# A graph layer on one core: the rows of x by a transpose, and lists, flag and bases moved

## The chip, the cores and the metric

The kernel runs on one core of a Trainium2 chip. The metric is the device time of one execution in microseconds (us); the time before is a median of three runs. Beside these runs there is one profiled execution with its own time and trace.

## The reference

There are 50,000 nodes with 128 numbers each (x) and 1,650,000 edges, sorted by their target. Each edge takes the row of its source, sends it through one of two linear maps (chosen by the edge's type), and the results are added up at the target. Then follow the node's own linear map, a relu, the sum with x, and a normalisation of each row:

```python
msg = jnp.where((edge_types == 0)[:, None], Xs @ W_data.T + b_data, Xs @ W_control.T + b_control)   # Xs = X[src]
agg = jax.ops.segment_sum(msg, dst, num_segments=X.shape[0])
out = relu(agg + (X @ W_self.T + b_self))
return _layernorm(X + out)
```

## The kernel before, in words

The sum over edges comes first and the linear maps after it, since both are linear. The edges are cut into 503 blocks of some 3,284. A block's edges end in a window of 112 nodes, whose first node is the block's base. Three ways bring the source rows of a block into SBUF:

- 24 chunks of 128 edges are gathered by POOL (GpSimd), one indirect DMA each (`gathers`, L464). Their lists of row numbers come from `fill`, which DVE runs five blocks ahead (`RAHEAD`). The rows land in a pool of ten buffers `y` of six chunks each.
- 128 edges are fetched as single rows, one DMA of 512 B each, half by SP's queue and half by ACT's (`single_rows`, L440). The row offsets are loaded into registers, 32 at a time (L435), and the rows are fetched two blocks ahead (`AHEAD`) into `yx`.
- Up to 84 edges are loops from a node to itself. They are left out of the lists and added from the window's own columns `xT` (`left_out_*`, L336 to L361).

For each chunk DVE makes a one-hot matrix over target and type (`onehot`, L401) and counts (`counts`, L409), and PE multiplies it with the rows into `acc` (L483, L489). DVE adds `acc` into one of three buffers `sums` (`add`, L499), which is carried from block to block with a shift (`begin_sums`, L512). When a block's sum is complete, `layer` multiplies it with the weights on PE into `po` (L517 to L520), `moments` takes relu and the sum with x on DVE (`h`, L525) and the moments (L527, L529), `root` takes the square root on ACT (L534), and `store` normalises (L540, L542) and writes the rows out by SP's queue (L543).

The order is written out by hand (`manual_schedule`): each engine runs its instructions in the order in which the loop over blocks issues them, and a DMA is issued in its queue's order. In an iteration b the loop first calls `window(b + 3)`, which reads the base of that block into a register of SP (L387) and loads the 112 rows `xw` (L393) and the same nodes' columns `xT` (L395, from a transposed copy of x). Then come the block's four passes of six chunks, and between them `layer(b - 1)`, `moments(b - 1)`, `onehot(b + 2)`, `counts(b + 2)`, `store(b - 1)`, `fill(b + 5)` and `single_rows(b + 2)`.

Before the loop, three weights are loaded, transposed on PE (L910) and copied (L911). Their buffers `w_sb` are given back, and the tiles that `straight` allocates next reuse the memory. `idx0`, the list of block 0, is the first DMA of SP (L116). After the loop a flag is computed (L618 to L640): it says whether the edges were as regular as this path assumes. All engines read it (L919), and only if it is above zero does a slower general path run. In the execution shown it does not run.

Of the kernel before, what the change touches and what calls it, by code (L numbers as in the profile page):

```python
# [11 lines left out]
F32 = mybir.dt.float32  # L12
# [4 lines left out]
ALU = mybir.AluOpType  # L17
# [5 lines left out]
N = 50000  # L23
D = 128
# [60 lines left out]
def straight(ctx, tc, c, x, x_t, src_t, dst_t, etype_t, src_f, dst_f, etype_f, src_x, dst_first, first_p, out):  # L85
# [38 lines left out]
    num_ps, rank_no_ps = small[:, :2 * W], small[:, 2 * W:2 * W + F]  # L124
    lists = [small[:, 2 * W + F + i * FILL:][:, :FILL] for i in range(2)]
    sums_at = [small[:Q * F, 2 * W + F + 2 * FILL + i:][:, :1] for i in range(2)]
    nc.vector.tensor_copy(num_ps, num)

    ones_b = keep.tile([P, P], BF16, name="ones_b")
    nc.vector.memset(ones_b, 1.0)  # L130
# [1 line left out]
    below = keep.tile([P, P], BF16, name="below")  # L132
    nc.gpsimd.affine_select(out=below, in_=ones_b, pattern=[[1, P]], compare_op=ALU.is_gt, fill=0.0,
                            base=0, channel_multiplier=-1)
    rank_no = keep.tile([P, F], F32, name="rank_no")
    nc.vector.tensor_scalar(rank_no, num[:, :F], -LOOP, None, op0=ALU.add)
    nc.vector.tensor_copy(rank_no_ps, rank_no)
# [243 lines left out]

    idxs = {0: idx0}
    bys, pcs, zs, pls, bases, ats, ys = {}, {}, {}, {}, {}, {}, {}
    ohs, cnts, accs, xws, xTs, pos, hs, mvs, sds = {}, {}, {}, {}, {}, {}, {}, {}, {}

    def base_of(b):
        return nc.values_load(base_i[0:1, b:b + 1], engines=[SP], min_val=0, max_val=N - B,  # L387
                              skip_runtime_bounds_check_because="it was clamped to this")

    def window(b):  # L390
        at = bases[b] = base_of(b)
        xw = stp.tile([B, D], F32, name="xw", bufs=5)
        nc.sync.dma_start(xw, x[bass.ds(at, B), :])  # L393
        xT = stp.tile([P, B], F32, name="xT", bufs=5)
        nc.sync.dma_start(xT, x_t[:, bass.ds(at, B)])  # L395
        xws[b], xTs[b] = xw, xT

    def onehot(b):
        g, i = divmod(b, GB)
# [13 lines left out]

    ROW_SLOTS = AHEAD + 2
    TURN = S // 2
    LOAD = TURN // 1
    RANGE = dict(min_val=0, max_val=(N - 1) * ROW, skip_runtime_bounds_check_because="where a node's row is")
    x_bytes = x.rearrange("n d -> (n d)").bitcast(U8)[None, :]
    fetched = [[tc.alloc_semaphore(f"fetched{j}_{i}") for i in range(ROW_SLOTS)] for j in range(2)]
# [5 lines left out]
            ats[b] = stp.tile([1, X], I32, name="at_x", bufs=AHEAD + 2)  # L425
            nc.vector.tensor_scalar(ats[b], one_g[g][:, i * X:(i + 1) * X], float(ROW), None, op0=ALU.mult)

    def single_rows(b, q, part):

        if q == 0 and part == 0:  # L430
            ys[b] = stp.tile([S, Q, D], F32, name="yx", bufs=ROW_SLOTS)
        both = []
        for j, (eng, dma) in enumerate(((SP, nc.sync), (ACT, nc.scalar))):
            at = j * TURN + part * LOAD
            _, rows = nc.values_load_multi_w_load_instructions(  # L435
                ats[b][0:1, q * S + at:q * S + at + LOAD], engines=[eng], **RANGE)
            both.append([(dma, fetched[j][b % ROW_SLOTS], at + k, row) for k, row in enumerate(rows)])
        for pair in zip(*both):
            for dma, sem, k, row in pair:
                copy = dma.dma_start(ys[b][k:k + 1, q, :].bitcast(U8), x_bytes[:, bass.ds(row, ROW)])  # L440
                copy.then_inc(sem, 16)
                tc.no_tile_sem_insts.add(copy.ins.name)
                tc.add_to_no_dep_group(f"single{b}", copy.ins)
# [69 lines left out]

    def layer(b):
        a = sums[b % RING]
        po = ps_o.tile([B, D], F32, name="po")
        nc.tensor.matmul(po, xTs.pop(b), c["wselfT"], start=True, stop=False)  # L517
        nc.tensor.matmul(po, a[0:3, 2, :B], bias, start=False, stop=False)  # L518
        for t in range(2):
            nc.tensor.matmul(po, a[:, t, :B], c["wmsgT"][:, t * D:(t + 1) * D], start=False, stop=t == 1)  # L520
        pos[b] = po

    def moments(b):
        h = stp.tile([B, D], F32, name="h")
        nc.vector.scalar_tensor_tensor(h, pos.pop(b), 0.0, xws.pop(b), op0=ALU.max, op1=ALU.add)  # L525
        st = stp.tile([B, 6], F32, name="st")
        nc.vector.bn_stats(st, h)  # L527
        mv = stp.tile([B, 2], F32, name="mv")
        nc.vector.bn_aggr(mv, st)  # L529
        hs[b], mvs[b] = h, mv  # L530
# [6 lines left out]
    def store(b):  # L537
# [4 lines left out]
        nc.vector.tensor_scalar(o, hs.pop(b), mv[:, 0:1], rstd, op0=ALU.subtract, op1=ALU.mult)  # L542
        nc.sync.dma_start(out[bass.ds(bases.pop(b), B), :], o)  # L543

    for b in range(1, AHEAD + 1):
        offsets(b)
    columns(0)
# [6 lines left out]
    for b in range(1, RAHEAD):  # L554
        fill(b)
        left_out_columns(b)
        left_out_matrix(b)
        if b < AHEAD:
            onehot(b)
            counts(b)  # L560
            for q in range(Q):
                for part in range(1):
                    single_rows(b, q, part)
        if b == 1:
            clear_sums()
    for b in range(NBLK + 1):
        if b + 3 < NBLK:
            window(b + 3)
        g, i = divmod(b, GB)
        if i == 0 and g + 1 < GROUPS:  # L570
            load_edges(g + 1)
        if i == 3 and g + 1 < GROUPS:
            spread_out(g + 1)
        if i == 4 and g + 1 < GROUPS:
            spread_in(g + 1)
        if b > 0:
            add(b - 1, steps_of(b - 1)[-1])
        if b < NBLK:
            begin_sums(b)
        last = steps_of(b)[-1:]  # L580
        for q, (step, ks) in enumerate(passes_of(b)):
            if ks:
                products(b, step, ks)
            if q == 0 and b > 0:
                layer(b - 1)
            if q == 1:
                left_out_numbers(b + 1)
            if q == 3:
                left_out_columns(b + RAHEAD)
            if ks and step not in last and ks[-1] == chunks_of(b, step)[-1]:  # L590
                add(b, step)
            if q == 0 and b > 0:
                moments(b - 1)
            if q == 0 and b + AHEAD < NBLK:
                onehot(b + AHEAD)
            if q == 1 and b > 0:
                root(b - 1)
            if q == 2 and b > 0:
                store(b - 1)
            if q == 1 and b + AHEAD < NBLK:  # L600
                counts(b + AHEAD)
            if q == 2 and i == 2 and g + 1 < GROUPS:
                columns(g + 1)
            if q == 2:
                left_out_rows(b + 1)
                if b + RAHEAD < NBLK:
                    fill(b + RAHEAD)
            if q == 3:
                left_out_matrix(b + RAHEAD)
                offsets(b + AHEAD + 1)  # L610
            if q % 2 == 0 and not plain(b + AHEAD):
                single_rows(b + AHEAD, q // 2, 0)


    ones = keep.tile([P, 1], F32, name="ones")
    nc.vector.memset(ones, 1.0)
    mm = keep.tile([P, 2], F32, name="mm")
    nc.vector.tensor_reduce(mm[:, 0:1], stats[:, :, 0, :], AX.XY, ALU.min)  # L618
    nc.vector.tensor_reduce(mm[:, 1:2], stats[:, :, 1, :], AX.XY, ALU.max)
    bad = keep.tile([P, 3], F32, name="bad")  # L620
    least = keep.tile([P, 1], F32, name="least")
    nc.vector.tensor_reduce(least, loops, AX.X, ALU.min)
    nc.vector.tensor_scalar(bad[:, 2:3], least, float(F), None, op0=ALU.is_lt)
    nc.vector.tensor_scalar(bad[:, 0:1], mm[:, 0:1], 0.0, None, op0=ALU.is_lt)
    nc.vector.tensor_scalar(bad[:, 1:2], mm[:, 1:2], float(W), None, op0=ALU.is_ge)
    gap = keep.tile([1, 3], F32, name="gap")
    nc.vector.tensor_reduce(gap[:, 0:1], shift, AX.X, ALU.min)
    nc.vector.tensor_reduce(gap[:, 1:2], shift, AX.X, ALU.max)
    nc.vector.tensor_scalar(gap[:, 0:1], gap[:, 0:1], 0.0, None, op0=ALU.is_lt)
    nc.vector.tensor_scalar(gap[:, 1:2], gap[:, 1:2], float(B), None, op0=ALU.is_gt)  # L630
    pb = ps_o.tile([B, D], F32, name="po")
    nc.tensor.matmul(pb[:3, 0:1], bad, ones, start=True, stop=True)
    both = keep.tile([3, 1], F32, name="both")
    nc.vector.tensor_copy(both, pb[:3, 0:1])
    pc = ps_o.tile([B, D], F32, name="po")
    nc.tensor.matmul(pc[:1, 0:1], both, ones[:3, 0:1], start=True, stop=True)
    nc.vector.tensor_copy(gap[:, 2:3], pc[:1, 0:1])
    total = keep.tile([1, 1], F32, name="total")
    nc.vector.tensor_reduce(total, gap, AX.X, ALU.add)
    nc.vector.tensor_copy(c["bad"], total)  # L640


def general(ctx, tc, c, x, src, dst, etype, out):
# [221 lines left out]
def gnn_resnorm(  # L865
# [35 lines left out]
    nc.vector.memset(eps, EPS)  # L901
    wmsgT = const.tile([P, 2 * D], F32, name="wmsgT")
    wselfT = const.tile([P, D], F32, name="wselfT")
    with tc.tile_pool(name="wts", bufs=2) as wts, \
            tc.tile_pool(name="wts_ps", bufs=2, space=bass.MemoryType.PSUM) as wts_ps:
        for w, o in ((w_data, wmsgT[:, :D]), (w_ctrl, wmsgT[:, D:]), (w_self, wselfT)):
            w_sb = wts.tile([P, D], F32, name="w_sb")
            nc.scalar.dma_start(w_sb, w)
            pw = wts_ps.tile([P, D], F32, name="pw")
            nc.tensor.transpose(pw, w_sb, ident)  # L910
            nc.scalar.copy(o, pw)  # L911
# [63 lines left out]
```

## Time and profile before

| | us |
|---|---|
| median of three runs | 24,102.25 |
| the three runs | 24,035.24, 24,102.25, 24,134.87 |
| the profiled execution's own time | 15,118.55 |
| its span | 15,116.8 |
| POOL busy, DVE busy | 11,399.7, 10,626.1 |
| PE busy, granted TensorE clock | 8,042.1, 0.544 |

The span runs from the first instruction to the last. Busy time counts instructions of the engine itself and neither its waits nor the issue of DMAs by SP and ACT. In the rows of instruction groups, the number after the bar is the busy time, then the mean duration in ns, then the idle time of the engine just before those instructions and what ended most of it. The profiled execution is much shorter than the runs shown, and nothing in the page says why; both are given wherever it matters.

### The profile page before, as it was taken

To read this page: it belongs to the slowest core of one execution; us is meant where nothing else is said; L and a number is where in the kernel's file an instruction comes from. 1 tells how busy PE (TensorE), PEld (TensorE's weight loads), DVE (VectorE), ACT (ScalarE), POOL (GpSimd) and SP (SyncE) were. 2 spreads that over 40 slices of the span, in tenths; PEclk is the share of its full clock that TensorE was granted. 3 is DMA by queue.
4 is the path that set the end of the run, shared out by engine and by line. 5 is a ranking of instruction groups with operands and counts; after the bars stand their busy time and mean duration, and the time that the engine had idled before them with its cause. 6 is when DMAs were issued, how large, how long until landed. Compare 5 with 4: busy or idle time off the path is not lost.

```text
span 15116.8 us, 243274 instructions
## 1 busy us (share of the span) xinstructions
PE 8042.1 (53%) x34836; PEld 6872.7 (45%) x34837; DVE 10626.1 (70%) x13316; ACT 151.7 (1%) x509; POOL 11399.7 (75%) x12071
## 2 busy tenths in 40 slices
PE   3555555555555555555555555555555555555555
PEld 3444444444444444444444444444444444444444
DVE  8776676767767767776676767767777676767765
ACT  0000000000000000000000000000000000000000
POOL 7777777777777777777777777777777777777777
PEclk7555555555555555555555555555555555555555
DMA  2332222222222222222222222222222222222222
GB/s 66 64 65 64 65 65 64 64 65 65 64 65 64 65 64 65 64 65 64 65 64 65 64 65 64 65 64 65 65 64 64 65 65 64 64 65 65 64 65 58
DMA packets 753407, 970.59 MB, mean 64 GB/s; under 512 B 355317, under 2 KB 552100, under 8 KB 751779
## 3 DMA queue, kind: packets, MB, share of 16 engines
q0 software_dynamic: 385968, 791.19, 21.5%
q1 hardware_dynamic: 301244, 146.99, 4.0%
q10 hardware_dynamic: 64566, 16.74, 0.6%
q14 instruction: 1345, 11.01, 0.2%
q8 instruction: 284, 4.65, 0.1%
HBM read 924.76 MB, written 29.02 MB: 63 GB/s over the span
## 4 chain that ended last, share of the span: by engine, by line
POOL 59%; issue 20%; PE 9%; DMA 6%; DVE 4%; ACTq 1%; SPq 0%; POOLq 0%; PEldq 0%; ACT 0%; PEld 0%; DVEq 0%
POOL y L464 59%; DMA y<-in_x,idx 6%; PE acc L483 6%; PE po L520 2%; PE po L518 1%; PE po L517 1%; ACTq L440 1%; DVE cnt L409 0%; DVE by L329 0%; DVE h L525 0%; DVE st L527 0%; DVE m L310 0%; DVE new L313 0%; DVE v_new L317 0%; DVE old L326 0%
## 5 line engine op out<-in xcount | busy, mean ns | idle before, releaser
L464 POOL DMA_INDIRECT y<-in_x,idx x12048 | 11385.9, 945 | 3683.0 <-issue 3573.7
L483 PE MATMUL acc<-oh,y 128*128 128x120 f32 x24122 | 5753.1, 428 | 6277.9 <-PEq L471 6263.0
L483 PEld LDWEIGHTS acc<-oh,y 128*128 128x128 f32 x24122 | 5208.8, 325 | 6688.2 <-PEq L471 6663.4
L409 DVE TENSOR_REDUCE cnt<-oh 128x240 bf16<-128x3120 f32 x503 | 2914.2, 5794 | 0.1
L525 DVE SCALAR_TENSOR_TENSOR h<-po,xw 112x128 f32<-112x128 f32 x503 | 146.7, 292 | 2994.7 <-PE po L520 2937.1
L401 DVE TENSOR_TENSOR oh<-col,small 128x3120 f32<-128x3120 f32 x503 | 1695.9, 3372 | 0.0
L329 DVE TENSOR_REDUCE by<-old 128x84 bf16<-128x1092 f32 x501 | 1066.7, 2129 | 17.4
L499 DVE TENSOR_TENSOR sums<-acc,sums 128x180 f32 x1006 | 347.2, 345 | 960.0 <-PE acc L492 900.9
L489 PE MATMUL acc<-oh,yx 64*128 64x120 f32 x2004 | 769.3, 485 | 7.4 <-PEq L449 7.4
L310 DVE TENSOR_TENSOR m<-rk,small 128x1092 f32<-128x1092 f32 x501 | 647.3, 1292 | 17.1
L313 DVE TENSOR_TENSOR new<-m,small 128x1092 f32<-128x1092 f32 x501 | 647.1, 1292 | 17.1
L317 DVE TENSOR_REDUCE v_new<-new 128x26 f32<-128x1092 f32 x501 | 646.8, 1291 | 17.1
L326 DVE TENSOR_TENSOR old<-m,small 128x1092 f32<-128x1092 f32 x501 | 643.2, 1284 | 0.0
L489 PEld LDWEIGHTS acc<-oh,yx 64*128 64x128 f32 x2004 | 492.5, 303 | 215.9 <-issue 204.6
L520 PE MATMUL po<-wmsgT,sums 128*112 128x128 f32 x2012 | 527.7, 408 | 0.0
L336 PE MATMUL small<-ones_b,by 128*84 128x1 bf16 x501 | 113.0, 225 | 733.2 <-DVE by L329 728.7
L520 PEld LDWEIGHTS po<-wmsgT,sums 128*112 128x112 f32 x2012 | 383.7, 262 | 111.9 <-issue 97.8
L336 PEld LDWEIGHTS <-by 128*84 128x84 bf16 x501 | 73.7, 147 | 791.0 <-DVE by L329 787.1
L518 PE MATMUL po<-bias,sums 3*112 3x128 f32 x1006 | 356.9, 452 | 0.2 <-DVE sums L499 0.2
L517 PE MATMUL po<-wselfT,xT 128*112 128x128 f32 x1006 | 316.9, 419 | 0.0
L512 DVE TENSOR_TENSOR sums<-pl,sums 128x336 f32<-128x336 f32 x501 | 254.3, 508 | 85.0 <-DVE sums L499 83.9
L534 ACT ACTIVATE sd<-mv,eps 112x1 f32<-112x1 f32 x503 | 148.3, 295 | 14831.2 <-PE acc L483 6098.9
(115 smaller groups left out, 3640.2 us busy)
## 6 DMA issues: line engine op xcount, KB each, us to landing
yx<-in_x ACTq DMA_DIRECT2D x32064, 0.5 KB
yx<-in_x SPq DMA_DIRECT2D x32064, 0.5 KB
y<-in_x,idx POOLq DMA_INDIRECT x12048
xw<-in_x SPq DMA_DIRECT2D x503, 56.0 KB
xT<-in_x_t SPq DMA_DIRECT2D x503, 56.0 KB
out<-o SPq DMA_DIRECT2D x503, 56.0 KB
vf_all<-vd SPq DMA_DIRECT2D x51, 420.0 KB
s<-in_src_t SPq DMA_DIRECT2D x51, 130.0 KB
```

Of the source, the lines that this page charges most:

```text
L310: nc.vector.tensor_tensor(m, rk_g[g][:, i, :, None].to_broadcast([P, C1, F]), rank_no_ps[:, None, :].to_broadcast([P, C1, F]), op=ALU.is_e ...
L313: nc.vector.tensor_tensor(new.rearrange("p (q r) f -> p q r f", r=R1), m.rearrange("p (q r) f -> p q r f", r=R1), vf.rearrange("p (q f) -> ...
L317: nc.vector.tensor_reduce(v, new, AX.X, ALU.add)
L326: nc.vector.tensor_tensor(old, m, cb[:, :, None].to_broadcast([P, C1, F]), op=ALU.mult)
L329: nc.vector.tensor_reduce(by, old.rearrange("p (q r) f -> p q f r", r=R1), AX.X, ALU.add)
L401: nc.vector.tensor_tensor(oh, col_g[g][:, i, :, None].to_broadcast([P, C1, 2 * W]), num_ps[:, None, :].to_broadcast([P, C1, 2 * W]), op=AL ...
L409: nc.vector.tensor_reduce(cnt, ohs[b].rearrange("p (q r) w -> p q w r", r=R1), AX.X, ALU.add)
L464: copy = nc.gpsimd.indirect_dma_start(out=y[:r, k % PASS, :], out_offset=None, in_=x, in_offset=bass.IndirectOffsetOnAxis(ap=idxs[b][:r, c ...
L483: nc.tensor.matmul(acc[:, :2, :].rearrange("p t w -> p (t w)"), y[:r, k % PASS, :], ohs[b][:r, column(k), :], start=k == of_step[0], stop= ...
L489: nc.tensor.matmul(acc[:, :2, :].rearrange("p t w -> p (t w)"), ys[b][:, q, :], ohs[b][:S, q * R1 + R, :], start=False, stop=True)
L518: nc.tensor.matmul(po, a[0:3, 2, :B], bias, start=False, stop=False)
L520: nc.tensor.matmul(po, a[:, t, :B], c["wmsgT"][:, t * D:(t + 1) * D], start=False, stop=t == 1)
```

## The change

`window` no longer loads `xw`. `layer` has PE transpose `xT` against the identity into a second half of `po`'s PSUM tile, and `moments` copies that half to SBUF as `h` and adds it there. The base of a block is loaded to a register together with those of the four blocks after it. The weights are loaded into one tile of their own that is not given back, so that `idx0` need not wait for them, and DVE's copy of `num` comes after its first memset. The flag's computation is now a function, called ahead of the last block's iteration instead of after the loop. The parameter `part` of `single_rows`, which had one value, is gone.

```diff
     def window(b):
-        at = bases[b] = base_of(b)
-        xw = stp.tile([B, D], F32, name="xw", bufs=5)
-        nc.sync.dma_start(xw, x[bass.ds(at, B), :])
+        if b % BASES == 0:
+            n = min(BASES, NBLK - b)
+            _, regs = nc.values_load_multi_w_load_instructions(
+                base_i[0:1, b:b + n], engines=[SP], min_val=0, max_val=N - B,
...
+            bases.update({b + i: at for i, at in enumerate(regs)})
+        at = bases[b]
         xT = stp.tile([P, B], F32, name="xT", bufs=5)
         nc.sync.dma_start(xT, x_t[:, bass.ds(at, B)])
-        xws[b], xTs[b] = xw, xT
+        xTs[b] = xT
...
     def layer(b):
         a = sums[b % RING]
-        po = ps_o.tile([B, D], F32, name="po")
-        nc.tensor.matmul(po, xTs.pop(b), c["wselfT"], start=True, stop=False)
+        both = ps_o.tile([B, 2, D], F32, name="po")
+        po, xT = both[:, 0, :], xTs.pop(b)
+        nc.tensor.transpose(both[:, 1, :], xT, c["ident"])
+        nc.tensor.matmul(po, xT, c["wselfT"], start=True, stop=False)
...
     def moments(b):
         h = stp.tile([B, D], F32, name="h")
-        nc.vector.scalar_tensor_tensor(h, pos.pop(b), 0.0, xws.pop(b), op0=ALU.max, op1=ALU.add)
+        po = pos.pop(b)
+        nc.vector.tensor_copy(h, po[:, 1, :])
+        nc.vector.scalar_tensor_tensor(h, po[:, 0, :], 0.0, h, op0=ALU.max, op1=ALU.add)
...
     for b in range(NBLK + 1):
+        if b == NBLK - 1:
+            find_bad()
         if b + 3 < NBLK:
             window(b + 3)
...
-    with tc.tile_pool(name="wts", bufs=2) as wts, \
-            tc.tile_pool(name="wts_ps", bufs=2, space=bass.MemoryType.PSUM) as wts_ps:
-        for w, o in ((w_data, wmsgT[:, :D]), (w_ctrl, wmsgT[:, D:]), (w_self, wselfT)):
-            w_sb = wts.tile([P, D], F32, name="w_sb")
+    w_all = const.tile([P, 3, D], F32, name="w_all")
+    with tc.tile_pool(name="wts_ps", bufs=3, space=bass.MemoryType.PSUM) as wts_ps:
+        for i, (w, o) in enumerate(((w_data, wmsgT[:, :D]), (w_ctrl, wmsgT[:, D:]), (w_self, wselfT))):
+            w_sb = w_all[:, i, :]
             nc.scalar.dma_start(w_sb, w)
```

`find_bad` holds the flag's instructions unchanged, but that its two small products write to the first half of the wider PSUM tile.

More of the change, by code (lines that the diff above doesn't have):

```diff
@@ L126, in straight @@
     sums_at = [small[:Q * F, 2 * W + F + 2 * FILL + i:][:, :1] for i in range(2)]
-    nc.vector.tensor_copy(num_ps, num)
     ones_b = keep.tile([P, P], BF16, name="ones_b")
@@ L134, in straight @@
                             base=0, channel_multiplier=-1)
+    nc.vector.tensor_copy(num_ps, num)
     rank_no = keep.tile([P, F], F32, name="rank_no")
@@ L383, in straight @@
     bys, pcs, zs, pls, bases, ats, ys = {}, {}, {}, {}, {}, {}, {}
[L384 to L388, printed above, removed]
+    ohs, cnts, accs, xTs, pos, hs, mvs, sds = {}, {}, {}, {}, {}, {}, {}, {}
+    BASES = 5
     def window(b):
-        at = bases[b] = base_of(b)
-        xw = stp.tile([B, D], F32, name="xw", bufs=5)
-        nc.sync.dma_start(xw, x[bass.ds(at, B), :])
+        if b % BASES == 0:
+            n = min(BASES, NBLK - b)
+            _, regs = nc.values_load_multi_w_load_instructions(
+                base_i[0:1, b:b + n], engines=[SP], min_val=0, max_val=N - B,
+                skip_runtime_bounds_check_because="it was clamped to this")
+            bases.update({b + i: at for i, at in enumerate(regs)})
+        at = bases[b]
         xT = stp.tile([P, B], F32, name="xT", bufs=5)
         nc.sync.dma_start(xT, x_t[:, bass.ds(at, B)])
-        xws[b], xTs[b] = xw, xT
+        xTs[b] = xT
     def onehot(b):
@@ L415, in straight @@
     TURN = S // 2
-    LOAD = TURN // 1
     RANGE = dict(min_val=0, max_val=(N - 1) * ROW, skip_runtime_bounds_check_because="where a node's row is")
@@ L426, in offsets, with single_rows @@
             nc.vector.tensor_scalar(ats[b], one_g[g][:, i * X:(i + 1) * X], float(ROW), None, op0=ALU.mult)
-    def single_rows(b, q, part):
-        if q == 0 and part == 0:
+    def single_rows(b, q):
+        if q == 0:
             ys[b] = stp.tile([S, Q, D], F32, name="yx", bufs=ROW_SLOTS)
@@ L433, in single_rows @@
         for j, (eng, dma) in enumerate(((SP, nc.sync), (ACT, nc.scalar))):
-            at = j * TURN + part * LOAD
+            at = j * TURN
             _, rows = nc.values_load_multi_w_load_instructions(
-                ats[b][0:1, q * S + at:q * S + at + LOAD], engines=[eng], **RANGE)
+                ats[b][0:1, q * S + at:q * S + at + TURN], engines=[eng], **RANGE)
             both.append([(dma, fetched[j][b % ROW_SLOTS], at + k, row) for k, row in enumerate(rows)])
@@ L520, in layer @@
             nc.tensor.matmul(po, a[:, t, :B], c["wmsgT"][:, t * D:(t + 1) * D], start=False, stop=t == 1)
-        pos[b] = po
+        pos[b] = both
     def moments(b):
         h = stp.tile([B, D], F32, name="h")
-        nc.vector.scalar_tensor_tensor(h, pos.pop(b), 0.0, xws.pop(b), op0=ALU.max, op1=ALU.add)
+        po = pos.pop(b)
+        nc.vector.tensor_copy(h, po[:, 1, :])
+        nc.vector.scalar_tensor_tensor(h, po[:, 0, :], 0.0, h, op0=ALU.max, op1=ALU.add)
         st = stp.tile([B, 6], F32, name="st")
@@ L543, in store, with find_bad @@
         nc.sync.dma_start(out[bass.ds(bases.pop(b), B), :], o)
+    def find_bad():
+        ones = keep.tile([P, 1], F32, name="ones")
+        nc.vector.memset(ones, 1.0)
+        mm = keep.tile([P, 2], F32, name="mm")
+        nc.vector.tensor_reduce(mm[:, 0:1], stats[:, :, 0, :], AX.XY, ALU.min)
+        nc.vector.tensor_reduce(mm[:, 1:2], stats[:, :, 1, :], AX.XY, ALU.max)
+        bad = keep.tile([P, 3], F32, name="bad")
+        least = keep.tile([P, 1], F32, name="least")
+        nc.vector.tensor_reduce(least, loops, AX.X, ALU.min)
+        nc.vector.tensor_scalar(bad[:, 2:3], least, float(F), None, op0=ALU.is_lt)
+        nc.vector.tensor_scalar(bad[:, 0:1], mm[:, 0:1], 0.0, None, op0=ALU.is_lt)
+        nc.vector.tensor_scalar(bad[:, 1:2], mm[:, 1:2], float(W), None, op0=ALU.is_ge)
+        gap = keep.tile([1, 3], F32, name="gap")
+        nc.vector.tensor_reduce(gap[:, 0:1], shift, AX.X, ALU.min)
+        nc.vector.tensor_reduce(gap[:, 1:2], shift, AX.X, ALU.max)
+        nc.vector.tensor_scalar(gap[:, 0:1], gap[:, 0:1], 0.0, None, op0=ALU.is_lt)
+        nc.vector.tensor_scalar(gap[:, 1:2], gap[:, 1:2], float(B), None, op0=ALU.is_gt)
+        pb = ps_o.tile([B, 2, D], F32, name="po")[:, 0, :]
+        nc.tensor.matmul(pb[:3, 0:1], bad, ones, start=True, stop=True)
+        both = keep.tile([3, 1], F32, name="both")
+        nc.vector.tensor_copy(both, pb[:3, 0:1])
+        pc = ps_o.tile([B, 2, D], F32, name="po")[:, 0, :]
+        nc.tensor.matmul(pc[:1, 0:1], both, ones[:3, 0:1], start=True, stop=True)
+        nc.vector.tensor_copy(gap[:, 2:3], pc[:1, 0:1])
+        total = keep.tile([1, 1], F32, name="total")
+        nc.vector.tensor_reduce(total, gap, AX.X, ALU.add)
+        nc.vector.tensor_copy(c["bad"], total)
     for b in range(1, AHEAD + 1):
@@ L561, in straight @@
             for q in range(Q):
-                for part in range(1):
-                    single_rows(b, q, part)
+                single_rows(b, q)
         if b == 1:
@@ L611, in straight @@
             if q % 2 == 0 and not plain(b + AHEAD):
[L612 to L640, printed above, removed]
+                single_rows(b + AHEAD, q // 2)
 def general(ctx, tc, c, x, src, dst, etype, out):
```

## The prediction

> **What bounds the kernel now.** I read the busy times on the page first, then the wait view of POOL, then one block on the timeline, then the wait view of DVE and SP's own queue, because a busy share alone does not say which engine is waited for.
>
> ```profile
> PE 8042.1 (53%) x34836; PEld 6872.7 (45%) x34837; DVE 10626.1 (70%) x13316; ACT 151.7 (1%) x509; POOL 11399.7 (75%) x12071
> L464 POOL DMA_INDIRECT y<-in_x,idx x12048 | 11385.9, 945 | 3683.0 <-issue 3573.7
> L525 DVE SCALAR_TENSOR_TENSOR h<-po,xw 112x128 f32<-112x128 f32 x503 | 146.7, 292 | 2994.7 <-PE po L520 2937.1
> ```
>
> No engine looks full, but POOL's idle time in the second row has the releaser "issue": the engine waited for nothing that the profile shows. The waits of POOL and of DVE say so gather by gather (columns: total us, times, longest us):
>
> ```profile
> POOL y L464 <- issue: 3577.7, 11718, 0.3
> POOL y L464 <- PE acc L483: 11.7, 29, 3.2
> DVE h L525 <- PE po L520: 2937.1, 494, 9.1
> ```
>
> POOL's busy 11,399.7 us plus these 3,577.7 us are 14,977 of 15,116.8 us, 99.1%. So a gather costs 0.945 + 0.303 = 1.248 us whatever else runs, and a block of 24 gathers 29.95 us; 503 blocks of that are the kernel. Of the 11,718 gaps none is above 0.3 us, so nothing is ever late for POOL: the row buffers (ten of six chunks) and the lists made five blocks ahead cover everything. DVE stands idle 2,937/503 = 5.8 us in a block before h. That is its reserve.
>
> SP is the second tightest. One block of its queue, and two gathers of POOL beside it:
>
> ```profile
> 5023.65 0.94 POOL L464 DMA_INDIRECT y<-in_x,idx  x1 [0.30 <-issue]
> ...
> 5024.90 0.94 POOL L464 DMA_INDIRECT y<-in_x,idx  x1 [0.30 <-issue]
> ```
> ```profile
> 5021.11 0.34 SPq L543 DMA_DIRECT2D out<-o  x1
> 5023.70 10.26 SPq L440 DMA_DIRECT2D yx<-in_x  x32
> 5034.73 0.32 SPq L393 DMA_DIRECT2D xw<-in_x  x1
> 5035.23 0.36 SPq L395 DMA_DIRECT2D xT<-in_x_t  x1
> 5037.63 10.63 SPq L440 DMA_DIRECT2D yx<-in_x  x32
> 5052.14 0.34 SPq L543 DMA_DIRECT2D out<-o  x1
> ```
> ```profile
> L387 SPq TENSOR_LOAD <-base_i x503: 280/542/772, 28.5 to 14997.2; - x168
> L435 SPq TENSOR_LOAD <-at_x x1002: 1866/2077/2373, 32.9 to 15014.4; - x167
> ```
>
> SP's own work in a block: 64 single rows at 0.33 (10.63/32) = 21.3 us, two register loads of 32 offsets at 2.08 = 4.2, one base load 0.54, xw 0.50 to the start of xT, xT 0.43, out 0.47: about 27.4 us of 29.95. It keeps up with 2.5 us to spare.
>
> **The two times.** The profiled execution took 15,118.55 us (span 15,116.8), the median of the runs shown is 24,102.25, 1.594 times that, and the three runs lie within 0.41% of each other. The profile does not show where the other 8.98 ms is. I make the sums on the profiled time and carry them over as a share, and keep as a rival that the hidden time sits on one queue.
>
> **What the Trainium skill says.** (1) "SBUF — State Buffer", section "SBUF: two separate sides": a DMA issued from POOL has its descriptors written by GpSimd, and a VectorE operation in a two-port mode locks GpSimd out meanwhile. The trace agrees in its first 20 us, where gathers beside large SBUF-to-SBUF operations of DVE take up to 1.64 us instead of 0.94. (2) "VectorE: DVE Perf Modes", section "Why PSUM operands drop a tier": a PSUM operand rules the two-port modes out and leaves fp32 at the single rate. So the new copy, which reads PSUM, should not lock POOL; in the trace, gathers beside the PSUM-reading h (0.29 us) stay at 0.94. No run here shows a PSUM-to-SBUF copy of that size.
>
> **The change part by part.**
> *First list first.* SP's first DMA (L116) waited 2.5 + 2.3 + 0.6 = 5.4 us for the weights' buffers, whose memory it reuses; the weights now have a buffer of their own, so it can issue at about 0.8 instead of 6.23 us. All of SP's first loads are queued behind it, so they move with it: first_i from 9.63 to 4.2, DVE's first use of it from 13.44 to about 8.1, the list of block 1 from 41.7 to 36.3. POOL starts 5.4 us earlier and waits for that list as before (1.7 us). Gain 5.4 us. The copy of num moved behind a memset saves DVE a wait of 5.6 us that lies under the wait for first_i: nothing.
> *Flag ahead of the last block.* DVE's last store ends at 15,101.55 and the flag (L618 to L640, with two tiny products on PE) at 15,104.48; after that come 12.3 us of reading the flag and branching, which stay. Gain 2.9 us, between 0 and 3. The moved work stands ahead of the last block, where DVE idles 14.2 us for PE (15,068.0 to 15,082.2) while POOL has 20 gathers left. Its two products are queued on PE behind the products of the block before, so DVE's next sums (L499) come about 1 us later, and the layer that needs them starts only at 15,088.4: hidden; if that cover were gone, up to 2.9 us back.
> *xw gone.* 503 loads of 56 KB, with 0.50 us of SP each. DMA engines are 25% busy and SP has 2.5 us to spare: nothing while POOL is the bound. What is late next is the offsets' load, which waits for DVE.
> *Transpose on PE.* One fp32 transpose a block. The nearest row is the weights' (L910), 0.447 us at full clock plus a weight load of 0.18; at the granted 0.544 that is at most 0.82 + 0.33 us. PE has 14 us idle in a block. It stands ahead of the self product in the chain to h, so h comes 0.5 to 1.1 us later; what waits behind h on DVE is the comparison of block b+2, whose use is two blocks off. Cost nothing, as long as it stays under the 5.8 us.
> *Copy out of PSUM.* 503 copies of 112x128. Nearest rows: 0.285 us for 128x120 into PSUM, 0.155 for one element out of it. I take 0.29, DVE 21.1 to 21.4 us a block: nothing. Its effect on POOL is the one unknown: from below 0 (the PSUM rule above; a gain is excluded, since the copy takes no work from POOL), from above the worst gather seen beside DVE, 1.64 - 0.94 = 0.70 us, 352 us in all. I take 0.
> *Five bases a load.* Thirty-one more registers cost 2.08 - 0.54 us, 0.05 each, so five cost 0.74, or 0.15 a block against 0.54: 0.4 us of SP a block, nothing under POOL.
> Sum: -8.3 us of 15,118.55, to 15,110; a share of 0.055%, on the median 24,089 us.
>
> **The rivals.**
> *POOL's pace stands (no change):* the sum above. For it, the 11,718 equal gaps. Against it, that the runs shown are longer than any such pace explains, by 8.98 ms.
> *SP is the bound in the runs shown (faster).* They spend 24,102/503 = 47.9 us a block. SP at 27.4 us was within 9% of POOL; if its issue is what takes longer there, SP sets the end, and its removed work counts. That is 0.50 (xw) + 0.39 (bases) = 0.9 of 27.4 us, 3.3%: 24,102 x 0.967 = 23,310 us. For it, the small reserve, and single issues of the same kind did take up to 0.71 us on this queue. Against it, their median is 228 ns from the first thousand us of the profile to the last.
> *The copy locks POOL out (slower).* If the PSUM copy stops descriptor writing, each of the 503 costs up to 0.70 us: +352 us, 24,454 us. It decides from 0.24 us a block (0.5% of 24,102 is 120 us). Against it stands the PSUM rule and the clean gathers beside h; for it, that no such copy has been seen, and that gathers did suffer beside other DVE operations. The same sign has the case that DVE or PE, not POOL, sets the unprofiled pace; then 0.29 + 0.82 us a block, 558 us, would show.
> That the change doesn't do what it says is not one: in the order of instructions xw's load and four of five base loads are gone from SP, and the transpose and copy are there.
>
> **How the numbers follow.** A change under 0.5% is about what a measurement of this kernel can't tell from none. Chances: POOL's pace stands 0.42; SP 0.36; slower 0.22. The likeliest gives 24,089, by itself 24,000 to 24,180 (the spread of the runs). The range reaches to both rivals: 23,250 to 24,480; left out are the 558 us and a return of the runs to the profiled time, together under 0.2.
>
> **What would show it.** Right: POOL's gathers 0.945 us with gaps of 0.3 and a span near 15,108; first gather near 3 us; no DVE work of the flag after the last store; SP's block down by 0.9 us, with longer waits on DVE; DVE's wait before h near 5.5 us and not zero. Wrong: gathers above 1.0 us beside the new copy; a wait of DVE before h that has vanished; or a median down by some 3% at an unchanged profile, which would mean the bound of the timed runs is not the one in the trace.

## The result and the profile after

The kernel after takes 23,791.1 us (median of 4 runs, 23,746.84 to 23,824.91), the kernel before 24,111.88 us on the same chip (median of 4 runs, one more than stands above). The ratio is 0.9871 [0.9848, 0.9894]: **faster by 1.3%**, 320.8 us, or 0.64 us in each of 503 blocks. The medians of before differ by up to 1.8% between the chips used, so each kernel below is compared with runs of before on its own chip, and each ratio is to these.

The profiled execution of after took 23,746.84 us (span 23,745.1). It is one of the ordinary runs, and so its page shows what the first profile of before, with its 15,118.55 us, could not. Of its page, the busy times, the line of the chain by engine, and two groups:

```profile
PE 7049.0 (30%) x35339; PEld 6348.5 (27%) x35340; DVE 10836.4 (46%) x13819; ACT 151.4 (1%) x509; POOL 11390.3 (48%) x12071
...
SPq 55%; issue 35%; DVE 6%; PE 2%; DMA 1%; another core or an unknown queue 0%; ACTq 0%; PEldq 0%; DVEq 0%; PEld 0%; ACT 0%
...
L465 POOL DMA_INDIRECT y<-in_x,idx x12048 | 11376.6, 944 | 12270.0 <-PE acc L484 7453.6
...
L529 DVE COPY h<-po 112x128 f32<-112x128 f32 x503 | 146.7, 292 | 1758.7 <-PE po L523 1541.2
```

POOL's busy time is what it was, and one gather still takes 944 ns. But its idle time in the gathers' row has grown from 3,683.0 to 12,270.0 us, and 7,453.6 of that is ended by PE. The chain of work runs through SP's queue for 55% of the span. The waits of all engines (total us, times, longest us) give the order of cause:

```profile
PE acc L490 <- PEq L450: 10910.5, 461, 37.6
...
POOL y L465 <- PE acc L484: 7468.9, 560, 20.1
...
POOL y L465 <- issue: 3307.1, 10838, 0.5
...
DVE h L529 <- PE po L523: 1541.2, 467, 4.1
...
SPq L436 <- DVE sums L500: 238.9, 147, 2.2
```

Read it from the second line: POOL waits for PE to free a row buffer `y`. PE in turn waits at L450 (first line), which is its wait for the single rows of `yx`, up to 37.6 us at a time. SP, which issues half of those rows, waits for almost nothing. So by these waits the single rows set the pace, and POOL with its gathers is behind them. On the timeline of SP's queue one half's 32 rows take 22.94 us in one place and 18.71 in the next (10.26 and 10.63 in the first profile of before):

```profile
5003.59 22.94 SPq L441 DMA_DIRECT2D yx<-in_x  x32
5028.00 0.00 SPq L548 DMA_DIRECT2D out<-o  x1
5030.16 18.71 SPq L441 DMA_DIRECT2D yx<-in_x  x32
5049.05 0.36 SPq L397 DMA_DIRECT2D xT<-in_x_t  x1
```

The same stretch cut where POOL pauses (columns: the stretch, its length, then busy us and instructions of PE, PE's loads, DVE, ACT and POOL, the granted clock, the DMA share and GB/s):

```profile
5000.00:5006.70 6.70, 4.22 (x23) 3.95 (x24) 3.19 (x2) 0.30 (x1) 0.00 (x0) 0.54 0.07 15
5006.70:5023.90 17.20, 6.55 (x37) 5.70 (x36) 13.42 (x19) 0.00 (x0) 11.34 (x12) 0.70 0.19 48
5023.90:5039.30 15.40, 1.41 (x13) 1.22 (x11) 4.35 (x5) 0.00 (x0) 11.32 (x12) 0.70 0.20 52
5039.30:5052.00 12.70, 1.17 (x7) 0.90 (x8) 0.14 (x1) 0.29 (x1) 0.00 (x0) 0.50 0.15 39
```

I counted the instructions that SP's queue starts in each of these stretches, register moves and DMAs alike: 28, 32, 31 and 56, which is 4.2, 1.9, 2.0 and 4.4 per us. SP is slow where POOL issues gathers (second and third stretch, 12 each) and more than twice as fast where POOL has none. DVE is busy for 13.42 of 17.20 us in the second stretch and for 4.35 of 15.40 in the third, PE for 6.55 and 1.41, and SP is as slow in both: it goes with the gathers and not with DVE or PE. Over the whole span SP starts 2.10 per us beside gathers and 4.51 without them, ACT 1.88 and 4.58. (Where a stretch is cut moves these rates: cut exactly at the end of its last gather, they are 2.2 and 4.2 for SP, 1.9 and 4.3 for ACT.) In the slow stretch the starts stand at steps of about 0.70 us or twice that, for a move as for a DMA (starts in us, from the trace):

```
5013.28 DMA   5014.02 MOVE  5014.73 DMA   5016.13 MOVE
5016.86 DMA   5017.56 MOVE  5018.27 DMA   5019.70 MOVE
```

This is not one place only. In the whole trace 12,948 of SP's 69,750 starts follow the one before after 0.68 to 0.76 or 1.38 to 1.44 us, which makes 12.0 of the 23.7 ms; in the first profile of before it is 43 of 71,517.

This closes a ring: rows are slow while POOL gathers; POOL then runs out of row buffers because PE waits for rows; in POOL's pause the rows catch up. A block takes 47.2 us, some 30 of them with gathers and 17 without. In the first profile of before the gathers ran the whole time too, and SP started 4.77 per us, ACT 4.45: that one execution was free of the slowing. So gathers alone do not bring it about, and no run here leaves the gathers out; that they take part is read from the stretches in which it stands.

### The profile page after: what moved, and what is told of

Read it like the earlier page. It is cut to its first block, busy times and chain, and to the rows that moved or that the text cites. A ratio compares the mean times of both kernels' runs of the same rounds, so it can differ in the third digit from the quotient of the medians.

```text
span 23745.1 us, 242605 instructions
## 1 busy us (share of the span) xinstructions
PE 7049.0 (30%) x35339; PEld 6348.5 (27%) x35340; DVE 10836.4 (46%) x13819; ACT 151.4 (1%) x509; POOL 11390.3 (48%) x12071
## 4 chain that ended last, share of the span: by engine, by line
SPq 55%; issue 35%; DVE 6%; PE 2%; DMA 1%; another core or an unknown queue 0%; ACTq 0%; PEldq 0%; DVEq 0%; PEld 0%; ACT 0%
SPq L441 47%; SPq L436 6%; DVE cnt L411 2%; SPq L548 1%; DMA yx<-in_x 1%; PE acc L484 1%; PE acc L490 1%; SPq L397 1%; DVE by L329 0%; DVE new L313 0%; DVE m L310 0%; DVE v_new L317 0%; DVE oh L403 0%; PE po L523 0%; SPq L164 0%
## 5 line engine op out<-in xcount | busy, mean ns | idle before, releaser
L465 POOL DMA_INDIRECT y<-in_x,idx x12048 | 11376.6, 944 | 12270.0 <-PE acc L484 7453.6
L484 PE MATMUL acc<-oh,y 128*128 128x120 f32 x24122 | 5001.2, 392 | 15.6 <-issue 15.5
L484 PEld LDWEIGHTS acc<-oh,y 128*128 128x128 f32 x24122 | 4761.3, 301 | 17.0 <-issue 16.8
L490 PE MATMUL acc<-oh,yx 64*128 64x120 f32 x2004 | 631.6, 405 | 10973.0 <-PEq L450 10910.5
L490 PEld LDWEIGHTS acc<-oh,yx 64*128 64x128 f32 x2004 | 400.6, 248 | 11156.8 <-PEq L450 11024.4
L529 DVE COPY h<-po 112x128 f32<-112x128 f32 x503 | 146.7, 292 | 1758.7 <-PE po L523 1541.2
```

Of the source, the lines that this page charges most:

```text
L465: copy = nc.gpsimd.indirect_dma_start(out=y[:r, k % PASS, :], out_offset=None, in_=x, in_offset=bass.IndirectOffsetOnAxis(ap=idxs[b][:r, c ...
L484: nc.tensor.matmul(acc[:, :2, :].rearrange("p t w -> p (t w)"), y[:r, k % PASS, :], ohs[b][:r, column(k), :], start=k == of_step[0], stop= ...
L490: nc.tensor.matmul(acc[:, :2, :].rearrange("p t w -> p (t w)"), ys[b][:, q, :], ohs[b][:S, q * R1 + R, :], start=False, stop=True)
```

## The experiments

**The kernel before again** (label before_again, no edit), for a profile of an ordinary run.

> The kernel before, profiled once more, to see what its 24.1 ms are made of. SP theory: the time is near 24,110 us and this trace shows SP's single-row issues (L440) slowed, about 0.66 us each on average where the first profile had 0.33, with SP never waiting, and POOL waiting some 17 us in a block for row buffers that PE gives back late. POOL theory: each gather takes about 2.0 us (24,102/12,061) and SP waits for DVE as it did in the first profile.

Measured: 23,776.37 us against 23,782.25, ratio 1.0 [0.9991, 1.0009]. The waits of PE, POOL and SP, and SP's queue on the timeline:

```profile
PE acc L489 <- PEq L449: 10912.6, 455, 37.5
...
POOL y L464 <- PE acc L483: 7476.7, 538, 22.2
...
SPq L435 <- DVE sums L499: 434.4, 397, 1.9
```
```profile
5008.21 23.60 SPq L440 DMA_DIRECT2D yx<-in_x  x32
5033.94 0.01 SPq L543 DMA_DIRECT2D out<-o  x1
5036.07 16.75 SPq L440 DMA_DIRECT2D yx<-in_x  x32
5053.59 0.32 SPq L393 DMA_DIRECT2D xw<-in_x  x1
5054.13 0.36 SPq L395 DMA_DIRECT2D xT<-in_x_t  x1
```

The time that the first profile lacked, here 8.6 ms, lies in these waits: 32 rows take 23.60 and 16.75 us, POOL stands idle some 17 us a block beyond the usual 0.30 before each gather, and the gathers themselves stay at 0.947 us. SP starts 2.21 instructions per us beside gathers and 4.55 without. The change has nothing to do with the slow pace; the kernel before has it too, and in this profile its time is that of its timed runs. Note xw: from its start to that of xT are 0.54 us, against 0.50 in the fast profile. Of the 503 loads of xw, 450 stand where POOL pauses, at 0.53 us on average; the 53 beside gathers take 2.6.

**The parts, each alone.** xw_only takes the loads of `xw` away and puts the transpose and the copy in:

```diff
-        xw = stp.tile([B, D], F32, name="xw", bufs=5)
-        nc.sync.dma_start(xw, x[bass.ds(at, B), :])
+        nc.tensor.transpose(both[:, 1, :], xT, c["ident"])
+        nc.vector.tensor_copy(h, po[:, 1, :])
```

> The kernel before with only the xw load replaced by the transpose and the copy; bases, first list and flag as before. SP theory, at SP's unslowed price: 0.50 us of SP saved in each of 503 blocks, -250 us, 23,860 us (ratio 0.990). SP theory with the whole of SP's work stretched by 1.74: -440 us. Traffic theory (the gain is 28 MB less of DMA, not queue time): the whole -321 us, 23,790 us. POOL theory: no change.

Measured: 23,629.14 us, 0.994 [0.9927, 0.9954]. bases_only loads five bases at a time:

```diff
-        at = bases[b] = base_of(b)
+        if b % BASES == 0:
+            n = min(BASES, NBLK - b)
+            _, regs = nc.values_load_multi_w_load_instructions(
+                base_i[0:1, b:b + n], engines=[SP], min_val=0, max_val=N - B,
...
```

> The kernel before with only the five bases per register load. SP theory at the unslowed price: 0.39 us of SP a block, -196 us, 23,915 us (ratio 0.992); stretched by 1.74: -340 us. Traffic theory and POOL theory: no change, since not one byte less is moved and POOL is untouched.

Measured: 23,675.13 us, 0.996 [0.9947, 0.9974]. edges_only has the weights in one tile that is kept, and the flag ahead of the last block:

```diff
+        if b == NBLK - 1:
+            find_bad()
...
+    w_all = const.tile([P, 3, D], F32, name="w_all")
```

> The kernel changed, with xw's load and the single base loads put back: only the first list first and the flag ahead of the last block are left of the change. Both theories: -5.4 us at the start and -2.9 us at the end, ratio 0.9997, which no round can tell from 1; the first gather near 3 us in the trace instead of 8.4.

Measured: 23,759.09 us, 0.9991 [0.9983, 0.9999], 21 us less with an interval from 2 to 40 us, which holds the 8.3 foreseen. The three parts add up to 0.60 + 0.40 + 0.09 = 1.09%; the whole gave 1.29% on one chip and 1.12% [0.95, 1.28] on another. So what the change brings, it brings by what it takes off SP's queue; for the bases there is no other way, since they move no byte less, while for xw the 28 MB that are no longer moved were not separated from the queue. Each part brings little more than half of its work: 153 us/503 = 0.30 us for 0.50 of xw, 107/503 = 0.21 for 0.39 of the bases. The rest goes back to the rows, which took 39.7 us a block in before_again, 40.1 in xw_only and 40.0 in bases_only (each move or DMA counted from its start to the next start on the queue, in one profiled execution each).

**Transpose and copy twice** (twice, and twice_again beside after on another chip).

```diff
+        nc.tensor.transpose(both[:, 1, :], xT, c["ident"])
         nc.tensor.transpose(both[:, 1, :], xT, c["ident"])
...
+        nc.vector.tensor_copy(h, po[:, 1, :])
         nc.vector.tensor_copy(h, po[:, 1, :])
```

> The kernel changed, with the transpose on PE and the copy on DVE each done twice. My sum costed both at nothing: ratio to before as the kernel changed on the same chip, about 0.989. If they lie on the path that sets the end: 0.29 us of DVE and up to 0.82 us of PE a block, 146 to 558 us more, ratio 0.995 to 1.012. If the copy locks POOL out: gathers above 0.95 us beside it.

> The kernel changed once more, beside the same kernel with the added work doubled, so that both are held against the same runs of the kernel before. If the parts add up (0.994, 0.996 and 0.9991 alone), the ratio to before is near 0.989; the first measurement gave 0.987.

> The kernel changed with the transpose and the copy each done twice, now on one chip with the kernel changed. Added work hidden: the same ratio as the kernel changed, within 0.002. Added work on the path: 0.006 to 0.023 above it.

Measured: twice 23,759.12 us, 0.9822 [0.9808, 0.9835]. On the other chip after_again 23,477.27, 0.9888 [0.9872, 0.9905], and twice_again 23,434.9, 0.9871 [0.9855, 0.9888]. A second copy and transpose add no time: beside after_again the intervals overlap. On its chip twice lies even below both measurements of after (0.9871 and 0.9888), which were made on other chips; the runs do not show why. The gathers keep their duration: in after 497 of them overlap a copy, and these take 942 ns on average and 954 at most. Of the page of twice_again:

```profile
L465 POOL DMA_INDIRECT y<-in_x,idx x12048 | 11377.6, 944 | 11938.9 <-PE acc L484 7181.2
```

**Fewer rows on SP** (split28): SP fetches 28 of 64 rows of a half block, ACT 36.

```diff
+    TAKE = ((0, 28), (28, 36))
...
-            at = j * TURN
+            at, n = TAKE[j]
```

> The kernel changed, with 28 of 64 single rows on SP and 36 on ACT instead of 32 each (ACT's 36 in two register loads). If SP's queue alone sets the block: SP loses 8 rows at 0.64 us, 5.1 us a block, and ACT, which waits some 9 us a block now, becomes the bound near 44.5 us: ratio to before about 0.93. If SP and ACT share one limit while gathers run, nothing is gained by moving rows from one to the other: ratio as the kernel changed, about 0.99.

Measured: 22,707.8 us, 0.939 [0.9376, 0.9404]. The ratio includes the change; against after's 0.9871 and 0.9888, four rows fewer on SP in each half block bring about four times what the whole change brought. The block goes to 44.9 us; SP now has gaps above 2.6 us that come to about 2.4 us a block, and ACT, which had about 8.9 us of them in after, has next to none. The long wait of PE for single rows is gone from the list of waits, and one on ACT has come in:

```profile
DVE rstd L549 <- ACT sd L543: 4325.7, 273, 37.7
```

ACT's square root stands in the same queue as ACT's rows, and DVE waits for it. The serial work of SP's queue was the bound, and with this split the bound passes to the other queue.

**No single rows at all** (one_gather): POOL fetches the block's 128 remaining edges with a 25th gather.

```diff
-        for pair in zip(*both):
-            for dma, sem, k, row in pair:
-                copy = dma.dma_start(ys[b][k:k + 1, q, :].bitcast(U8), x_bytes[:, bass.ds(row, ROW)])
+        copy = nc.gpsimd.indirect_dma_start(
+            out=y, out_offset=None, in_=x,
+            in_offset=bass.IndirectOffsetOnAxis(ap=idxs[b][:, R:R + 1], axis=0))
```

> The kernel changed, with the 128 single rows of a block fetched by one more gather of POOL instead of 128 DMAs of SP and ACT. SP theory: SP and ACT have next to nothing left, POOL is the bound at 25 gathers of 1.248 us, 31.2 us a block, about 15,720 us (ratio to before about 0.66), and POOL waits for nothing. If it were POOL that is slow in the runs (2.0 us a gather): 25/24 of the time before, some 24,800 us.

Measured: 18,022.69 us, 0.7451 [0.7439, 0.7462]. This beats both kernels by a quarter, but it is not the time of POOL's pace that I expected. POOL still waits some 4.5 us a block. On the timeline, first PE's weight loads, then its products:

```profile
5024.48 0.29 PEld L467 LDWEIGHTS acc<-oh,yx 128*128 128x128 f32 x1 [1.81 <-issue]
5025.89 0.10 PEld L470 LDWEIGHTS <-to_row 128*128 128x128 bf16 x1 [1.11 <-issue]
```
```profile
5023.78 0.36 PE L467 MATMUL acc<-oh,yx 128*128 128x120 f32 x1 [2.18 <-issue]
5025.19 0.36 PE L467 MATMUL acc<-oh,yx 128*128 128x120 f32 x1 [1.06 <-issue]
5026.58 0.26 PE L470 MATMUL acc<-cnt,to_row 128*128 128x60 bf16 x2 [1.03 <-issue]
```

A product, a load, a product, a load: 23.78, 24.48, 25.19, 25.89, 26.58. These are again steps of 0.70 us, and each idle stretch before them has the releaser "issue". PE's queue shows the same step as SP's: in this trace 2,896 gaps between starts of loads and products have that length or twice it, 2.6 ms in all, against 94 in after and 41 in the first profile of before. That these steps are what keeps POOL waiting is likely, but not shown.

**Half the bytes** (half_gather): each gather fetches 64 of its 128 rows, and the other rows are left out of the sums.

```diff
-            r = LAST if b == NBLK - 1 and k == RCH - 1 else P
+            r = P // 2
```

> The kernel changed, with each chunk's gather fetching 64 of its 128 rows; the other rows of each chunk are left out of the sum. SP and ACT have the same work. If the gathers' data on the DMA engines is what slows SP's queue, SP gets on faster while gathers run (2.1 instructions per us there now, 4.5 beside none), and the block gets well shorter, about 38 us of 47.2, some 19,000 us. If POOL's making of descriptors slows it, the rate beside gathers stays at 2.1, and the time falls only as far as a gather of half the rows takes less of POOL. If neither matters and SP's queue is slow in itself, the time stays.

Measured: 23,899.54 us (two runs, 1% apart), 0.988 [0.9835, 0.9926], no different from after's 0.9871. Its queue of gathers and its gathers, from the page:

```profile
q0 software_dynamic: 385952, 395.99, 7.5%
...
L465 POOL DMA_INDIRECT y<-in_x,idx x12048 | 10911.9, 906 | 12767.9 <-PE acc L484 7402.0
```

The gathers move 396 MB instead of 791, and SP still starts 2.10 instructions per us beside them. So the slowing does not follow the bytes in flight. The packets are as many as before, so it may still hang on their number.

**One more instruction a row** (alu): offsets are held in numbers instead of bytes, so that SP and ACT each carry out one register operation more for every row.

```diff
-                copy = dma.dma_start(ys[b][k:k + 1, q, :].bitcast(U8), x_bytes[:, bass.ds(row, ROW)])
+                copy = dma.dma_start(ys[b][k:k + 1, q, :], x_flat[:, bass.ds(row, D)])
```

> The kernel changed, with the offsets of the single rows counted in numbers instead of bytes, so that each of the rows' DMAs on SP and ACT gets one register instruction more (0.04 us where nothing slows it). What slows SP beside the gathers falls either on each DMA or on each instruction. Per DMA: a row stays at about 1.4 us beside gathers and costs 0.08 us more elsewhere: about 50 us a block, ratio to the kernel changed 1.06. Per instruction: a row beside gathers costs three times 0.7 us, 2.1 us, so fewer rows get done there and the rest takes 6 us more: about 53 us a block, 1.13. If SP is not the bound: no change.

Measured: 26,978.03 us, 1.1354 [1.1335, 1.1373]. The queue of SP goes from 138.7 to 202.4 instructions a block with the same DMAs, and the time to 1.148 of after's on this chip, near the 1.13 foreseen for a slowing of each instruction and far from the 1.06 for one of each DMA. The waits of POOL:

```profile
POOL y L465 <- PE acc L484: 10898.9, 577, 34.4
```

A register operation that moves no data costs time. Of SP's queue in this trace, the added operation takes 298 ns to the next start on average beside gathers and 82 ns without them, so the slowing falls on the instructions of the queue and not on the DMA alone. It isn't one full step for each: beside gathers SP started 2.45 instructions per us here, a little more than the 2.10 of after, and its gaps of 0.70 us or twice that are 14,321, not many more than the 12,948 of after.

**The wait of PE for DVE taken out of one_gather** (late): in one_gather PE waits for DVE's `by`, while DVE waits for PE.

```profile
PE small L333 <- DVE by L326: 5781.0, 396, 22.4
```

In late, the columns and the matrix of the left-out edges are made a step later.

```diff
-            if q == 3:
-                left_out_columns(b + RAHEAD)
+                if b > 0:
+                    left_out_columns(b + RAHEAD - 1)
```

> The kernel with one more gather instead of single rows (0.745), with PE's count of left-out edges (L333) and what DVE makes of it put one block later, since there PE waits 11.6 us a block for DVE's last reduction and DVE then waits for PE. If this mutual wait is what keeps POOL idle 4.5 us a block: down to 31.2 us a block, 15,720 us, ratio 0.65. If PE's own slowed instructions beside the gathers are: little change, 0.74.

Measured: 17,864.35 us, 0.7522 [0.7509, 0.7534]; one_gather had 0.7451 on another chip. The waits of PE and DVE:

```profile
PE po L498 <- DVE sums L477: 4942.4, 402, 23.1
...
DVE sums L477 <- remote: 4702.0, 395, 27.9
...
PE acc L461 <- issue: 2706.9, 1969, 3.2
```

("remote" is a releaser that the profile does not tell.) The long wait for `by` is gone, and 4,942 us of waiting stand at the next place where PE needs DVE; the time hardly moved, from 18,022.69 to 17,864.35 us. The mutual wait was where lost time showed, and not what lost it.

## Where the prediction was right and where wrong, point by point

**What held.** The likeliest case was no measurable change, 24,089 us, and it did not happen; 23,791.1 lies below that case's own 24,000 to 24,180. It lies inside the full range, 23,250 to 24,480, because that range reached out to both rivals; with the account behind the likeliest case wrong, this is luck as much as foresight. Right are the costs of the added work, which it took as hidden. The gathers beside the new copy take 942 ns, which agrees with the rule that the prediction took from the Trainium skill ("VectorE: DVE Perf Modes", section "Why PSUM operands drop a tier"): an operand in PSUM keeps an operation out of the two-port modes. So the slower rival, the copy that locks POOL out, falls. Transposes and copies cost nothing even when doubled, which also speaks against the case in which PE or DVE sets the pace. The first gather starts at 3.24 us instead of 8.38, 5.1 us earlier for 5.4 foreseen, and after the last store (L547 at 23,738.79) no work of the flag follows.

**The step that failed** is "I make the sums on the profiled time and carry them over as a share". It gave the likeliest case to POOL's pace, on the strength of 11,718 equal gaps of 0.3 us in a profile when the runs to be predicted were 1.594 times as long. Under it the loads of `xw` and of the bases were priced at nothing, and alone they brought 0.30 and 0.21 us a block. That POOL has no other gaps is true of that execution only. In before_again 10,905 such gaps are there too, but beside them POOL stands idle some 17 us a block, mostly for a PE that waits for single rows. My argument against the rival, that the single issues' median is 228 ns throughout, was drawn from the same wrong execution, and the median is no measure at that: in after it is still 228 ns, while the starts lie 0.70 us apart for part of the time and the longest tenth of the durations begins at 697 ns instead of 229.

**The rival that held** is "SP is the bound in the runs shown", in its mechanism. Its size was 792 us, and 321 came: the mis-sized term is the share, 0.9 of 27.4 us applied to the whole time. That share supposes that everything on SP's queue is stretched alike, so that 0.9 us would be worth some 1.6. But only what stands beside gathers is stretched, and nine in ten loads of `xw` stood where POOL pauses, at 0.53 us. Unscaled, 0.9 us a block is 453 us, and of this the rows took a part back. An estimate comes near: the kernel after has 138.7 instructions a block on SP's queue instead of 142.2; 3.5 fewer at the 4.5 per us of POOL's pauses are 0.78 us a block, for 0.64 measured. It supposes that the gathers of a block keep their 30 us, so that what is taken away shortens the pause, where SP is fast.

**Signs that I named.** "A median down by some 3% at an unchanged profile, which would mean the bound of the timed runs is not the one in the trace" was the right kind of sign, at 1.3%; the profile, though, was not unchanged but had the timed runs' length. I had said that SP would wait longer for DVE; its wait at the offsets' load fell from 434.4 to 238.9 us. DVE's wait before h, foreseen near 5.5 us a block, is 1,541.2/503 = 3.1, and in before_again 2.9: it had shrunk with the slow pace already, and not by the change.

**What stays open.** The runs show that the slowing stands in the stretches with gathers, that it falls on register operations of SP's queue as on DMAs, that ACT's queue slows with it, that halving the bytes of the gathers leaves it as it is, and that without single rows steps of the same length stand on PE. They do not show what in the chip makes it, nor why one execution of before was free of it. Fewer gathers of the same rows, or gathers with fewer packets, were not tried.

## What to carry to other kernels

When the profiled execution and the timed runs differ by half, profile again before any reasoning on the bound: the engine that looks full may be full only in that execution. Read a queue by the starts of its instructions and not by their durations, since a queue can lose half its speed while their median stays where it was. An issue queue with thousands of small DMAs can set the pace as an engine can; here, moving an eighth of SP's rows to ACT (0.939) and then all rows into one more gather (0.745) brought far more than trimming what stood beside them (0.987).

## What the runs showed of the hardware

Beside POOL's indirect gathers, SP's queue started 2.1 instructions per us and ACT's 1.9, against 4.5 and 4.6 without gathers, with steps of 0.70 us and its double; in one execution of the same kernel before they started 4.77 and 4.45 beside gathers. Halving the rows of a gather shortened it only from 944 to 906 ns. The Trainium skill says that issuing DMAs from several engines "only saves the sequencer's issue time" ("Trainium Kernel Development and Optimization", section "Key Constraints"); the runs agree on what is saved and show that it can be what sets the time: with the DMA engines busy for 7 to 20% of the four stretches shown, moving an eighth of SP's rows to ACT took the ratio from 0.987 and 0.989 (other chips) to 0.939.
